# One pool of matrix buffers through four graph layers, with the next layer's masks requested at the last head

## The chip, the cores and the metric

The kernel runs on one core of a Trainium2 chip. The metric is the device time of one execution in microseconds (us). Timed runs before the change took 3488.3, 3495.0 and 3485.93 us; their median is 3488.3 us. One execution was also recorded with the hardware profiler. It took 3488.49 us, and its span from the first to the last instruction is 3486.7 us.

The engines are called as in the profile: PE multiplies matrices and transposes, DVE, ACT and POOL work on tensors elementwise, and SP only issues DMA transfers. Each of them carries out its own list of instructions in order; an instruction that waits for a semaphore holds back what is behind it in that list.

## The reference, cut to what matters

There are N = 3327 nodes with D = 512 features and a dense adjacency matrix. Four layers follow each other, each one with a normalisation and a ReLU ahead of it and a residual behind it:

```python
# layers 0, 1, 2: graph attention with 8, 4 and 8 heads
h = maximum(layernorm(x), 0)
Wh = h @ W                                        # per head
e = leaky_relu(s1[i] + s2[j], 0.2)                # s1 = Wh . a1, s2 = Wh . a2
e = where(adj[i, j] > 0, e, -9e15)                # layer 1: adj + identity, -inf
x = x + elu(softmax(e, axis=j) @ Wh)
# layer 3: mean over the neighbours
h = maximum(layernorm(x), 0)
agg = mask @ h / maximum(deg, 1)
x = x + relu(concat(h @ W_self + b_self, agg @ W_nb + b_nb) @ W_comb + b_comb)
```

## The kernel before, in words

**Attention without exponentials of a matrix.** A leaky ReLU has two slopes, so exp(e) of an edge is one of two products, each of a factor of the row i and a factor of the column j. Which one holds depends on the sign of s1[i] + s2[j]. So a head needs, for each block of 128 source nodes by 128 target nodes, two matrices of zeros and twos in fp8: the edges of one sign and those of the other. Those of one sign come from a compare of the score row with a value per partition (line 683 on ACT, for some blocks line 680 on DVE), combined bit by bit with the adjacency mask (line 687, `and`, on DVE). Those of the other sign are the mask without the first (line 689, `xor`). PE multiplies both with the rows of Wh, which are scaled with the factors of the column and split into three bf16 pieces (lines 794 and 797). In layer 1 (4 heads) one matrix serves after the other in the same buffer (line 822 flips it in place); some groups there are cast to fp32r (line 652: three groups at a time on ACT or DVE, tiles `ts` and `tv`) and multiplied at line 787, the others at line 790.

**Loops.** The 26 tiles of 128 nodes are taken in chunks of 4 target tiles (seven chunks, the last with 2). Within a chunk the loop runs over heads, within a head over five groups of source tiles (6, 6, 6, 4 and 4). For each chunk, head and group there is one pair of matrix buffers, called `tht` and `gt`. In layers 0 and 2 there are seven of each, 3072 bytes per partition; layer 1 has ten `tht`, used for both signs. At the end of a head DVE sums the pieces out of PSUM (lines 812 and 808), and lines 828 to 835 normalise into the tile `A`. After the last head of a chunk, `finish` does the ELU (lines 892, 893 on ACT, 894 on DVE), adds the residual on POOL (895) and stores the rows (896).

**The next layer's projection** is interleaved with the attention as hooks. A node tile goes through stages: normalise (lines 347, 351 on DVE, 352 to 354 on POOL, ReLU at line 359 on ACT), transpose on PE (line 138) with a copy out of PSUM on ACT (line 142), multiply with the weights (line 415; 490 for the last layer), exponentials (446, 449) and scaling (454), splitting into pieces (386, 390, 397, 399; in layer 1 also 470 and 473), and a store of the pieces by SP (line 551). Scores of a whole chunk are transposed and sent at lines 519 and 521. The last chunk's two tiles have no other chunk to hide behind: their stages stand at the joint between two layers. At the joints of layers 0 to 1 and 1 to 2 the kernel also multiplies two weight matrices for the last layer (class `Fusion`): POOL loads a block (line 183) into one of two `xt` buffers, PE transposes (138) and multiplies it (190), ACT copies the result back into that buffer (191), and POOL stores it to `X` (192). Line 204 multiplies the biases.

**Masks and scores.** SP loads the adjacency masks of a chunk (line 273), five tiles out of a pool of six buffers; it loads the score row of a head, broadcast over the partitions (line 695, two buffers), and the pieces of the next head (lines 733 and 739). Within a layer the next chunk's masks are requested one head ahead. The first masks of layers 1 and 2 and of the last stage are requested when that layer begins (lines 703 and 1028). The next layer's first score row is requested at the last head already (line 723).

**The last stage** (lines 1041 to 1057) multiplies the mask, cast to fp32r into one of six `mf` buffers (line 1044 on ACT, 1042 on DVE), with the projected rows `y2_0` to `y2_4`, each in two parts (line 1047), and adds the other terms. The `y2` tiles are loaded by POOL (line 868); `y2_0` has a pool of its own and is requested before layer 2 ends.

**What sets the order.** The kernel's program is written as if for one sequence; a scheduler of the tile framework then arranges the instructions of each engine, from its own estimate of when they can run, and puts in the semaphore waits that data and reused buffers need. `after(inst, name)` (line 145) adds an order without a wait. Tiles live in pools. The attention pools of the layers are opened one after the other at the same addresses, so the first tiles of a layer can wait for whichever tile of the former layer lay there. A scheduler's order for the changed kernel can therefore differ from the former one also far from the lines that were edited.

Of the kernel before, what the change touches and what calls it, by code (L numbers as in the profile page):

```python
# [25 lines left out]
F32 = mybir.dt.float32  # L26
# [11 lines left out]
P = 128  # L38
# [14 lines left out]
def tile_gnn(ctx: ExitStack, tc: tile.TileContext, x, adj, W0, a01, W1, al, ar, W2, a2,  # L53
# [209 lines left out]
    def mask_view(c, g):  # L263
        nt, nj = chunks[c][1], JG[g][1]
        m = mk.tile([P, PER * JM * P], FP8, name="m")
        return m[:, :nt * nj * P].rearrange("p (k j i) -> p k j i", k=nt, j=nj)

    def mask_tiles(c, self_loops=False):
        t0, nt = chunks[c]
        tiles, loops = [], []  # L270
        for g, (j0, nj) in enumerate(JG):
            v = mask_view(c, g)
            nc.sync.dma_start(v, maskd[c][g])
# [250 lines left out]
    def node_stages(L, t, get_x, pool, first=False):  # L524
# [24 lines left out]
        def send():  # L549
            for to, pt in L.to_store:  # L550
                nc.sync.dma_start(to, pt)
            L.to_store = []
            send_s1(L, t, pool, first)
# [138 lines left out]
    def score_rows(l, t0, nt, h):  # L692
# [3 lines left out]
        return v  # L696

    def attention(L, hooks, open_next, close):

        l = L.l  # L700
        H, DA, AO, HW = dims(l)
        DK = DA - 1
        masks = mask_tiles(0, l == 1) if l else masks0
        for c, (t0, nt) in enumerate(chunks):
# [3 lines left out]
            for h in range(H):  # L708
# [37 lines left out]
                for g in range(len(JG)):  # L746
                    if g in early:
                        pv, gv = early.pop(g)
                    else:

                        pt = mp.tile([P, PER * JM * P], FP8, name="tht", bufs=10 if l == 1 else 7)
                        gt = pt if l == 1 else mp.tile([P, PER * JM * P], FP8, name="gt", bufs=7)
                        pv, gv, words, steps = matrices(L, nt, h, g, s1v, masks[g], pt, gt)
                        for step in steps:
                            step()
                        if l == 1:
                            flip.append(words)
                    th[0].append(pv)
                    th[1].append(gv)
                R = mp.tile([P, PER, 2, DA], F32, name="R", bufs=1)  # L760
                deg = l == 0 and h == 0
# [162 lines left out]
    with tc.tile_pool(name="first", bufs=1) as fp:  # L924
# [47 lines left out]
        while hooks.small:  # L972
            hooks.small.pop(0)()
    A, R = [("A", D, F32, n) for n in A_BUFS], ("R", PER * 2 * 129, F32, 1)
    ab, gt, tht = ("ab", JM * 400, BF16, 7), ("gt", PER * JM * P, FP8, 7), ("tht", PER * JM * P, FP8, 7)
    tags = [[A[0], ("R", PER * 2 * 65, F32, 1), tht, ("tr", JM * P, BF16, 5), ("abx", 4 * 400, BF16, 4), gt],
            [A[1], ("ab", JM * 258, F32R, 7), R, ("ts", 2 * JM * P, F32R, 3), ("tv", 2 * 4 * P, F32R, 2), tht[:3] + (10,)],
            [A[2], ab, ("R", PER * 2 * 65, F32, 1), tht, gt]]
    hooks.masks = in_steps([mask_steps(ip, t, g) for t, g in order[20:]])
# [31 lines left out]
    with tc.tile_pool(name="agg", bufs=1, reuse_waits="tile") as op:  # L1011


        y2n = [(f"y2_{g}", nj * 2 * D, F32R, 1) for g, (_, nj) in enumerate(JG)]
        lay_out(op, ("y1", D, F32, 3), ("xo", D, F32, 3), ("o", D, F32, 3), y2n[4], ("gap", 40 * 1024, FP8, 1),
                y2n[3], ("mf", JM * P, F32R, 6), y2n[1], y2n[2])
        rows = {}
# [493 lines left out]
```

## Time and profile before

| What | us or share |
|---|---|
| median of the timed runs | 3488.3 |
| profiled execution, its own time | 3488.49 |
| span of the profiled execution | 3486.7 |
| mean granted clock of PE | 0.994 |
| busy: DVE | 2635.9 (76%) |
| busy: POOL | 625.9 (18%) |
| L683 on ACT, 2448 compares of form `gt` | 1448.3, 677 ns each |
| L687 / L689 on DVE, 557 of each | 448.0 / 446.9, 805 / 803 ns each |
| L1047 on PE, 1352 | 309.6 busy |

PE's matmuls are pipelined, so the duration of one (248 ns for line 794) is longer than the time from one start to the next; on the timeline line 794 and line 797 start every 84 ns, line 790 every 164 ns, line 1047 every 227 ns. An idle time in brackets on a timeline line is the time in which the engine did nothing before that line, with the instruction that ended it behind the arrow. "xN" says how often the instruction was repeated in the line. The granted clock is the share of full speed that the throttle allowed to PE.

Layer 0 runs until about 1180 us, layer 1 until about 2025 us, layer 2 until about 3142 us, and the last stage to the end.

### The profile page before, as it was taken

Reading aid. Unit: us, or ns where it says so; the run is one execution under the profiler, and the core shown is the slowest. Engines: PE = TensorE matmul, PEld = TensorE weight load, DVE = VectorE, ACT = ScalarE, POOL = GpSimd, SP = SyncE. Lnnn points to the kernel's source line nnn. Section 1 sums busy time; section 2 is a strip of 40 time slices with the busy share of each in tenths; the row PEclk is TensorE's granted clock in tenths of the full one; section 3 lists DMA queues with packets and bytes.
Section 4 is the critical chain, followed back from the end, with each engine's and each line's share of the span. In section 5 each row is a group of like instructions: output and inputs, shape, how many; then the busy total and the mean of one; then the engine's idle time right before and its main releaser. Section 6 shows DMA issues by size and latency. Waiting matters only on the chain. (4 is left out here: it accounts for less than half of the span.)

```text
span 3486.7 us, 77621 instructions
## 1 busy us (share of the span) xinstructions
PE 3419.4 (98%) x30751; PEld 3095.4 (89%) x30751; DVE 2635.9 (76%) x5227; ACT 2501.2 (72%) x4113; POOL 625.9 (18%) x858
## 2 busy tenths in 40 slices
PE   8899999999999999999999999999999999999999
PEld 6799999999999788888888879989898989886887
DVE  7888888888878799889988867867676768672221
ACT  6777888878878888988888767766676767572111
POOL 7601222112111202223223320000000001020000
PEclk9999999999999999999999999999999999999999
DMA  8799999999857887877777876655555555586331
GB/s 230 234 287 263 249 257 256 262 266 262 251 178 271 271 285 262 294 266 270 276 273 267 334 261 200 197 179 172 191 171 180 186 176 186 164 296 261 103 107 57
DMA packets 398117, 797.70 MB, mean 229 GB/s; under 512 B 112969, under 2 KB 221844, under 8 KB 397104
## 3 DMA queue, kind: packets, MB, share of 16 engines
q1 hardware_dynamic: 363890, 723.14, 65.3%
q0 software_dynamic: 28128, 62.42, 7.5%
q10 hardware_dynamic: 5726, 7.08, 0.6%
q8 instruction: 245, 4.01, 0.5%
q14 instruction: 128, 1.05, 0.1%
HBM read 663.59 MB, written 129.64 MB: 228 GB/s over the span
## 5 line engine op out<-in xcount | busy, mean ns | idle before, releaser
L683 ACT ACTIVATE gt<-s1b,ks 128x512 fp8e4<-128x512 f32 (+1 forms) x2448 | 1448.3, 677 | 376.0 <-PE acc L797 260.6
L794 PE MATMUL acc<-ab,tht 128*128 128x195 bf16 (+1 forms) x9112 | 1550.6, 248 | 5.9 <-DVE tht L687 4.6
L797 PE MATMUL acc<-ab,gt 128*128 128x195 bf16 (+1 forms) x9112 | 1549.8, 248 | 2.5 <-DVE gt L689 2.3
L797 PEld LDWEIGHTS <-gt 128*128 128x128 fp8e4 x10744 | 1052.0, 98 | 26.4 <-issue 18.2
L794 PEld LDWEIGHTS <-tht 128*128 128x128 fp8e4 x10744 | 1051.9, 98 | 23.0 <-DVE tht L687 9.1
L687 DVE TENSOR_TENSOR tht<-gt,m 128x768 uint32<-128x768 uint32 (+3 forms) x557 | 448.0, 805 | 103.0 <-ACT gt L683 99.4
L689 DVE TENSOR_TENSOR gt<-tht,m 128x768 uint32<-128x768 uint32 (+3 forms) x557 | 446.9, 803 | 9.4
L652 ACT CAST ts<-tht 128x1536 fp32r<-128x1536 fp8e4 x208 | 302.2, 1472 | 100.3 <-PE acc L787 93.8
L680 DVE TENSOR_SCALAR gt<-s1b,ns 128x512 fp8e4<-128x512 f32 (+1 forms) x446 | 223.8, 505 | 161.1 <-PE acc L797 160.3
L787 PE MATMUL acc<-ab,ts 128*128 128x258 f32 x2496 | 332.8, 289 | 1.6 <-DMA ab<-ab 1.5
L787 PEld LDWEIGHTS acc<-ab,ts 128*128 128x128 f32 x2496 | 312.0, 189 | 9.7 <-ACT e L893 1.9
L895 POOL TENSOR_TENSOR xt<-xt,e 128x512 f32<-128x512 f32 x72 | 120.7, 1676 | 1066.2 <-DVE e L894 1005.8
L683 ACT ACTIVATE tht<-s1b,ks 128x512 fp8e4<-128x512 f32 (+1 forms) x504 | 309.1, 681 | 0.7
L1047 PE MATMUL acc<-y,mf 128*128 128x512 f32 x1352 | 309.6, 391 | 0.0
L1047 PEld LDWEIGHTS acc<-y,mf 128*128 128x128 f32 x1352 | 253.6, 188 | 55.8 <-issue 0.5
L794 PE MATMUL acc<-abx,tht 128*128 128x195 bf16 (+1 forms) x1632 | 284.6, 248 | 3.4 <-DVE tht L687 3.3
L797 PE MATMUL acc<-abx,gt 128*128 128x195 bf16 (+1 forms) x1632 | 284.4, 248 | 3.2 <-DVE gt L689 1.6
L812 DVE TENSOR_REDUCE R<-acc 128x130 f32<-128x390 f32 x416 | 214.3, 554 | 89.8 <-PE acc L797 86.8
L1044 ACT CAST mf<-m 128x768 fp32r<-128x768 fp8e4 (+1 forms) x78 | 59.1, 762 | 243.2 <-PE acc L1047 231.4
L790 PE MATMUL acc<-ab,tht 128*128 128x387 bf16 x1248 | 223.8, 327 | 6.4 <-DMA ab<-ab 4.2
L787 PE MATMUL acc<-ab,tv 128*128 128x258 f32 x1664 | 218.2, 283 | 0.0
L787 PEld LDWEIGHTS acc<-ab,tv 128*128 128x128 f32 x1664 | 207.2, 189 | 0.6 <-DVE tv L652 0.2
(163 smaller groups left out, 3706.9 us busy)
## 6 DMA issues: line engine op xcount, KB each, us to landing
ab<-ab SPq DMA_DIRECT2D x333, 600.0 KB, 5.8
ab<-ab SPq DMA_DIRECT2D x112, 774.0 KB, 6.7
ab<-ab SPq DMA_DIRECT2D x112, 516.0 KB, 5.4
ab<-ab SPq DMA_DIRECT2D x112, 400.0 KB, 3.8
abx<-ab SPq DMA_DIRECT2D x110, 400.0 KB, 6.5
ab<-ab SPq DMA_DIRECT2D x56, 582.0 KB, 6.2
s1b<-s SPq DMA_DIRECT2D x120, 256.0 KB, 5.5
m<-mask SPq DMA_DIRECT2D x69, 384.0 KB, 4.0
```

The costliest lines, as they stand in the source:

```text
L652: (nc.scalar.copy if KIND[g] == "s" else nc.vector.tensor_copy)(t[:, :k1 - k0, :nj], th[a][g][:, k0:k1])
L680: nc.vector.tensor_scalar(gv[:, :, jj, :], s1v, L.ns2[:, j, h:h + 1], 2.0, op0=ALU.is_gt, op1=ALU.mult, saturate=False)
L683: nc.scalar.activation(gv[:, :, jj, :], s1v, AF.Relu, bias=L.ks2[:, j, h:h + 1], scale=BIG, saturate=False)
L687: nc.vector.tensor_tensor(pu, gu, mu, ALU.bitwise_and)
L689: nc.vector.tensor_tensor(gu, pu, mu, ALU.bitwise_xor)
L787: mm = nc.tensor.matmul(acc[k][:, :2 * DA], thr[g][:, k - ks[0], jj, :], ab[a][g][:, jj, :], start=(j == 0), stop=(j == NT - 1), skip_grou ...
L790: mm = nc.tensor.matmul(acc[k][:, :3 * DA], th[a][g][:, k, jj, :], ab[a][g][:, jj, :3 * DA], start=(j == 0), stop=(j == NT - 1), skip_grou ...
L794: nc.tensor.matmul(acc[k][:, :3 * DA + o], th[0][g][:, k, jj, :], ab[0][g][:, jj, :3 * DA + o], start=(j == 0), stop=False, skip_group_che ...
L797: mm = nc.tensor.matmul(acc[k][:, AO:AO + 3 * DA + o], th[1][g][:, k, jj, :], ab[0][g][:, jj, AO:AO + 3 * DA + o], start=False, stop=(j == ...
L812: nc.vector.tensor_reduce(R[:, k], v.rearrange("p a (s d) -> p a d s", s=3), AX.X, ALU.add)
L895: nc.gpsimd.tensor_add(xt, xt, e)
L1047: nc.tensor.matmul(acc[k], mf[:, jj, :], y2[g][:, jj, s, :], start=(j0 + jj == 0 and s == 0), stop=(j0 + jj == NT - 1 and s == 1))
```

## The change

All layers and the last stage take their matrices from one pool, `mats`, of ten buffers `th` of 3072 bytes per partition; it lies on the other side of the memory and is never closed until the end. In layers 0 and 2 the pairs count in a cycle of seven: five pairs take two `th` buffers each, and two pairs take one of two double buffers `tx` in the layer's own pool. Layer 1 uses the ten `th` only, and the last stage uses them as `mf`. The other tiles of the layers' pools and of the last stage's are laid out at other addresses. The masks of the next layer are requested at the last head of the last chunk, right after its matrices, in layers 0 and 1. The last stores of the next layer's pieces (line 551) are put behind the last of these mask requests in order.

```diff
+            lds.append(nc.sync.dma_start(v, maskd[c][g]).ins.name)
...
-                nc.sync.dma_start(to, pt)
+                st = nc.sync.dma_start(to, pt)
+                if "masks" in early:
+                    after(st, lds[-1])
...
+    pairs = [0, 0, 0]
...
-        masks = mask_tiles(0, l == 1) if l else masks0
+        masks = early.pop("masks") if l else masks0
...
-                        pt = mp.tile([P, PER * JM * P], FP8, name="tht", bufs=10 if l == 1 else 7)
-                        gt = pt if l == 1 else mp.tile([P, PER * JM * P], FP8, name="gt", bufs=7)
+                        s = PER * JM * P
+                        if l == 1:
+                            pt = gt = thp.tile([P, s], FP8, name="th", bufs=10)
+                        elif (pairs[l] + (4 if l == 0 else 0)) % 7 < 5:
+                            pt, gt = [thp.tile([P, s], FP8, name="th", bufs=10) for _ in range(2)]
+                        else:
+                            both = mp.tile([P, 2 * s], FP8, name="tx", bufs=2)
+                            pt, gt = both[:, :s], both[:, s:]
+                        pairs[l] += 1
...
+                if last and h == H - 1 and l < 2:
+                    early["masks"] = mask_tiles(0, l == 0)
...
-    tags = [[A[0], ("R", PER * 2 * 65, F32, 1), tht, ("tr", JM * P, BF16, 5), ("abx", 4 * 400, BF16, 4), gt],
-            [A[1], ("ab", JM * 258, F32R, 7), R, ("ts", 2 * JM * P, F32R, 3), ("tv", 2 * 4 * P, F32R, 2), tht[:3] + (10,)],
-            [A[2], ab, ("R", PER * 2 * 65, F32, 1), tht, gt]]
+    thp = main.enter_context(tc.tile_pool(name="mats", bufs=1, side="right", reuse_waits="tile"))
+    lay_out(thp, ("th", PER * JM * P, FP8, 10))
+    A, R, R1 = [("A", D, F32, n) for n in A_BUFS], ("R", PER * 2 * 65, F32, 1), ("R", PER * 2 * 129, F32, 1)
+    tx = ("tx", 2 * PER * JM * P, FP8, 2)
+    tags = [[A[0], R, ("tr", JM * P, BF16, 5), ("abx", 4 * 400, BF16, 4), tx],
+            [A[1], ("ab", JM * 258, F32R, 7), R1, ("ts", 2 * JM * P, F32R, 3), ("tv", 2 * 4 * P, F32R, 2)],
+            [("ab", JM * 400, BF16, 7), R, tx, ("gap", 800, FP8, 1), A[2]]]
...
-        lay_out(op, ("y1", D, F32, 3), ("xo", D, F32, 3), ("o", D, F32, 3), y2n[4], ("gap", 40 * 1024, FP8, 1),
-                y2n[3], ("mf", JM * P, F32R, 6), y2n[1], y2n[2])
+        lay_out(op, ("y1", D, F32, 3), ("xo", D, F32, 3), ("o", D, F32, 3), y2n[4], ("gap", 31136, FP8, 1),
+                y2n[1], y2n[2], y2n[3])
...
-                        mf = op.tile([P, JM, P], F32R, name="mf", bufs=6)
+                        mf = thp.tile([P, PER * JM * P], FP8, name="th", bufs=10).bitcast(F32R)
+                        mf = mf.rearrange("p (j i) -> p j i", j=JM)
```

Line numbers in the text are those of the kernel before.

More of the change, by code (lines that the diff above doesn't have):

```diff
@@ L266, in mask_view @@
         return m[:, :nt * nj * P].rearrange("p (k j i) -> p k j i", k=nt, j=nj)
+    lds = []
     def mask_tiles(c, self_loops=False):
@@ L272, in mask_tiles @@
             v = mask_view(c, g)
-            nc.sync.dma_start(v, maskd[c][g])
+            lds.append(nc.sync.dma_start(v, maskd[c][g]).ins.name)
             if self_loops:
@@ L973, in tile_gnn @@
             hooks.small.pop(0)()
-    A, R = [("A", D, F32, n) for n in A_BUFS], ("R", PER * 2 * 129, F32, 1)
-    ab, gt, tht = ("ab", JM * 400, BF16, 7), ("gt", PER * JM * P, FP8, 7), ("tht", PER * JM * P, FP8, 7)
-    tags = [[A[0], ("R", PER * 2 * 65, F32, 1), tht, ("tr", JM * P, BF16, 5), ("abx", 4 * 400, BF16, 4), gt],
-            [A[1], ("ab", JM * 258, F32R, 7), R, ("ts", 2 * JM * P, F32R, 3), ("tv", 2 * 4 * P, F32R, 2), tht[:3] + (10,)],
-            [A[2], ab, ("R", PER * 2 * 65, F32, 1), tht, gt]]
+    thp = main.enter_context(tc.tile_pool(name="mats", bufs=1, side="right", reuse_waits="tile"))
[5 more added lines that the diff above has]
+            [("ab", JM * 400, BF16, 7), R, tx, ("gap", 800, FP8, 1), A[2]]]
     hooks.masks = in_steps([mask_steps(ip, t, g) for t, g in order[20:]])
```

## The prediction

> **What bounds the kernel now.** I read the page first, then busy time by windows of 50 us, then PE's list of waits, then the timelines of PE, ACT and POOL at the three joints between layers. The page says that PE sets the time:
>
> ```profile
> PE 3419.4 (98%) x30751; PEld 3095.4 (89%) x30751; DVE 2635.9 (76%) x5227; ACT 2501.2 (72%) x4113; POOL 625.9 (18%) x858
> ...
> PE 41%; ACT 0%; DVE 0%; POOL 0%; issue 0%; POOLq 0%
> ```
>
> Of a span of 3486.7 us PE is busy 3419.4 (the first figure), so about 67 us is all that better order can win, and the chain of waits (last line) holds next to nothing but PE. The windows tell where the 67 us lie. Columns: stretch and length, then busy us of PE, PEld, DVE, ACT, POOL, then granted clock, DMA share, GB/s.
>
> ```profile
> 1150.00:1200.00 50.00, 46.96 (x380) 38.87 (x378) 31.46 (x82) 34.30 (x78) 9.74 (x16) 1.00 0.85 284
> 2000.00:2050.00 50.00, 42.93 (x234) 32.20 (x233) 29.61 (x58) 24.78 (x42) 17.25 (x27) 0.97 0.87 318
> 2100.00:2150.00 50.00, 50.00 (x597) 50.00 (x595) 39.25 (x77) 36.40 (x60) 0.00 (x0) 1.00 0.65 207
> 3150.00:3200.00 50.00, 48.71 (x175) 33.30 (x176) 8.53 (x19) 9.35 (x14) 4.24 (x9) 0.93 0.81 311
> ```
>
> The third is a middle of a layer: PE never idle. So are nearly all windows. PE idles 3.0 us at the joint of layers 0 and 1, 5.2 + 7.1 at that of 1 and 2, 2.1 + 1.3 at the last stage; also 25.3 between 50 and 350 us (start of layer 0) and about 8 after its last matmul. The clock column adds a second loss: 0.97 over 50 us is 1.5 us, 0.93 is 3.5 us. What ended PE's idle time:
>
> ```profile
> PE tp L138 <- ACT h L359: 12.1, 5, 8.9
> PE acc L794 <- DVE tht L687: 7.9, 4, 3.4
> PE acc L790 <- DMA ab<-ab: 4.2, 2, 2.6
> PE acc L790 <- DVE tht L687: 2.1, 1, 2.1
> ```
>
> The columns are total us, times, longest. Waits for `tht L687` are those for the first matrices of a layer, which the change can bring forward: one of 2.1 (layer 1) and the longest, 3.4 (layer 2).
>
> **Middle of the layers: 0.** Every engine issues as many instructions after as before, of the same shapes. Five of seven pairs in the shared pool and two in `tx` make the same seven pairs in flight as seven `tht` and seven `gt` did; layer 1 has ten as before. One semaphore more on each of the 557 pairs (row L687 x557), at the 17 ns of the shortest such row (POOL's semaphore instructions at L192), would be 9.5 us of a queue; it is hidden because ACT is ahead: before L683 it idles 376.0 us, 260.6 of them until PE gives a buffer back. Bounds 0 to +9.5; I take 0, by the PE rows without idle time.
>
> **Joint 0 to 1: +1.6.** Today ACT stands idle while layer 1's compares could run:
>
> ```profile
> 1166.08 2.89 ACT L683 ACTIVATE gt<-s1b,ks 128x256 fp8e4<-128x256 f32 x7
> 1179.02 1.07 ACT L142 COPY hT<-tp 128x512 f32<-128x512 f32 x2 [4.90 <-PE tp L138]
> 1192.86 3.77 ACT L683 ACTIVATE tht<-s1b,ks 128x512 fp8e4<-128x512 f32 x6
> ```
>
> The first is the last of layer 0, the third the first of layer 1: it waited behind relu and copies in ACT's order. In the order of the changed kernel 18 of these compares (3.77/6 = 0.63 us each, 11.3 us) stand between the first and the second line. From 1168.97, with two L470 (1.2), L521 (0.3) and some waiting of the L470s (1.3 today), ACT reaches L142 at about 1182. PE needs that copy for the Fusion's L190, which today starts at 1179.66 after 0.24 idle. So the 2.12 us stall at L790 goes, and one of about 2.5 us comes at L190. What is late next: DVE puts layer 1's L687 and L680 between the final L812 and L835, so A is ready about 3.6 us later; PE's transpose of h comes 2.5 later itself and today has 1.7 to spare, so that is nearly hidden. Three L652 casts (1.472 us each, page) then stand ahead of the second L142, and PE's last L415 waits about 1.5, less the ten more L790 (164 ns apart) that it can do first. Sum: -2.1 + 2.5 + 1.2 = +1.6; bounds -2 (L142 in time) to +5 (waits of 3.1 and 1.5 whole, and one drop of the clock at 2.5, the middle of the two losses above).
>
> **Joint 1 to 2: +1.3.** Masks of groups 1 to 4 are asked for on SP at about 2016.7, 5.5 us earlier, ahead of two L551 stores, which go 3.5 us later (the four requests) at no cost, since the load of their group waits for a later L551 at 2051.95 in any case. So L683, L680 and L687 run earlier. The 3.37 us stall goes. But POOL's order changes as well. Today:
>
> ```profile
> 2031.70 0.57 POOL L192 DMA_DIRECT2D X<-xt  x1
> 2034.34 0.26 POOL L354 TENSOR_SCALAR mv<-mv 128x1 f32<-128x1 f32 x1
> 2038.54 0.56 POOL L183 DMA_DIRECT2D xt<-in_L_gnn_W_nb_dram  x1 [1.77 <-PE tp L138]
> 2040.70 0.26 POOL L354 TENSOR_SCALAR mv<-mv 128x1 f32<-128x1 f32 x1
> ```
>
> L183 reloads the buffer that L192 stores, so it waits until that store has landed; POOL is in order, so L352 to L354 of the next tile wait behind it. Now only the second tile does. In the changed order the L183 stands before the first tile's L352 to L354, and a second one before the second's. Landing of L192:
>
> ```profile
> DMA to landing us min/median/max: 2.5/4.5/7.2
> ```
>
> With the median of 4.5, L183 goes at 2036.5, L354 ends near 2039 (about 1.6 from L352 to L354, an L192 of 0.6 between) and h near 2039.8, where PE today starts L138 at 2037.01 without waiting: a new idle of some 2.5 us. From there: L138 0.6, copy 0.7, L415 3.83, so the second L138 is done at 2045.2. Its h is ready at 2044.3 (the second L183 waits for a store of 2037.1 that lands at 2041.6). On ACT four L683, L446, L449 and one more L683 stand between that h and L142 (5 x 0.63 + 0.2 = 3.4), so the copy ends at 2048.2 and PE's second L415 starts there; today it starts at 2046.94. That is +1.3, with the 3.37 us stall gone and its time spent elsewhere. L808 to L835 end 1.8 us later too, behind L687 and L689 (0.95 each), which the wait for X covers. Bounds by the same chain: landings of 2.5 bring L415 to 2044, -3; two landings of 6.3, the store's own today, +5; a clock drop more costs 1.5 to 3.5 above that.
>
> **Joint 2 to 3: -1.3.** ACT idles 12.47 us before L892 at 3143.41. The last stage's casts (L1044 six times, L1042 four times) fit there, since `mf` now comes from a pool that is free as layer 2 ends. Ten L1047 (0.227 us apart, 2.27 us) come between the transposes, where PE idles 2.09 + 0.68 + 0.62 = 3.4. They need y2_0, whose load at L868 was issued at 3138.93 and landed at 3150.1, so the first three wait as long as h does today, and hold up L138 by 0.7. Bounds: +3 (y2_0 later beside three mask loads that are now earlier) to -5 (idle 3.4 and some of the clock's 3.5 gone).
>
> **Start of layer 0 and the rest: 0.** One L689 comes before the last L812, which takes a 1.5 us stall and lengthens a 0.8 one; the third row of scores is issued about 6 us later, behind W loads, and ACT has up to seven pairs in hand (1.4 heads of 17.5 us) to hide it. Without that cover it costs up to 5; bounds -3 to +5. The stalls on `ab` (4.2, 1.5) and the 8 us at the end stay, as SP's order there stays.
>
> Sum: 0 + 1.6 + 1.3 - 1.3 + 0 = +1.6. The profiled execution took 3488.49 us (the span and 1.8 around it), 0.2 above the median of 3488.3. Forecast 3488.5 + 1.6 = **3490.1**.
>
> **The clock.** The rows: 0.97 and 0.93 in windows with idles of 1.9 to 3.4 us, 1.00 in the one with 2.12. The Trainium skill, "TensorE: Matmul & The Clock Gate", Part 1, says the rate halves after idle gaps over about 3.4 us. By it only the 3.37 us stall would be at risk, and taking it away would bring an estimated 1.7 us besides (half of 3.4), so 3488.4. The window with 0.93 holds no idle longer than 2.09 us, so the rows speak against that threshold; I count a stall of 2 us or more, old or new, as one that may drop the clock, expect as many drops after as before, and keep 3490.1.
>
> **Rivals.** *All as wished*: stalls 2.12 + 3.37 + 2.09 + 0.68 + 0.62 = 8.9 go, nothing new comes, and the clock keeps 1.5 + 3.5: -13.9, so 3474.6. For it: ACT has the idle time. Against it: the new places of L683 and L183 in queues that are in order. *Queues cost more* (slower): the same work ahead of what PE waits for, at L142 on ACT and L183 on POOL, at the upper bounds +5 and +5 + 3.5, with the last stage at 0: +13.5, so 3502.0. It decides from where X's stores take over 6 us to land and both new idles drop the clock; below that the loss stays under 10 us. *It does nothing*: each earlier matrix meets a wait of the same end (h, y2_0, X): 3488.5.
>
> **Chances.** Forecast 0.46 (3484 to 3497), nothing 0.12, all as wished 0.19, queues 0.23. A run of this kernel tells no change from about 0.3%, 10.5 us. So faster 0.19, same 0.58, slower 0.23. The range takes in most of both rivals: 3475 to 3503.
>
> **What would show it.** At 0 to 1, the 2.12 at L790 gone and an idle PE before L190: right; L190 at 1179.7 and no stall after: my joint was too dear. At 1 to 2, L138 waiting for h with L183 ahead of L352 on POOL; if L183 doesn't wait there, the gain is real. At 2 to 3, L1047 between the transposes, ended by y2_0's DMA. Any idle PE in a middle window would refute the zero there and make the forecast wrong by up to 9.5.

## The result: 0.66% slower, 10 us beyond the range

| | before | after |
|---|---|---|
| median of six timed runs each, us | 3489.91 | 3513.01 |
| lowest to highest, us | 3485.93 to 3495.0 | 3508.88 to 3515.22 |
| after / before, 95% interval | | 1.0066 [1.0056, 1.0077] |
| profiled execution / its span, us | 3488.49 / 3486.7 | 3510.98 / 3509.2 |
| PE idle (span less busy), us | 67.3 | 77.9 |

In the kernel after, lines move down: the compare L683 is L687, L680 is L684, `and` L687 is L691, `xor` L689 is L693, L794/L797 are L809/L812, L790 is L805, L617 is L621, L828 is L843, L352 to L354 are L354 to L356, L359 is L361, L415 is L417, L490 is L492, L1047 is L1065, L868 is L883. The experiments' kernels are off by a few lines more. The page of the kernel after, its busy engines, the shares of its chain of waits, and the group of the last stage's matmuls:

```profile
PE 3431.3 (98%) x30751; PEld 3099.2 (88%) x30751; DVE 2629.8 (75%) x5227; ACT 2502.3 (71%) x4113; POOL 639.3 (18%) x858
...
PE 40%; DVE 0%; POOL 0%; ACT 0%; issue 0%; POOLq 0%
...
L1065 PE MATMUL acc<-y,th 128*128 128x512 f32 x1352 | 315.5, 395 | 3.4 <-DVE mv L353 3.4
```

PE still sets the time, with the same 30751 matmuls. It is busy 11.9 us longer for them, and 5.9 of those are in the last group, which was 309.6 before: the same 1352 matmuls take longer, which is no waiting at all. What ended PE's idle time (total, times, longest):

```profile
PE acc L809 <- DVE th L691: 10.5, 3, 7.3
...
PE mm L417 <- ACT hT L142: 4.3, 4, 2.8
PE mm L190 <- ACT hT L142: 3.9, 2, 3.6
...
PE acc L805 <- DMA ab<-ab: 2.4, 2, 2.0
```

The waits for layer 2's and layer 1's first matrices (3.4 and 2.1) are gone as wished. New are one of 7.3 for a matrix, and waits for the copy L142. The windows of the kernel after (columns as in the prediction):

```profile
150.00:200.00 50.00, 41.43 (x444) 39.60 (x444) 34.10 (x75) 37.84 (x66) 10.32 (x16) 0.90 0.87 268
1150.00:1200.00 50.00, 46.36 (x410) 40.29 (x408) 38.94 (x99) 44.79 (x102) 7.93 (x13) 0.93 0.82 273
2050.00:2100.00 50.00, 43.05 (x328) 35.21 (x329) 27.05 (x61) 30.09 (x55) 10.44 (x17) 0.93 0.59 203
2100.00:2150.00 50.00, 50.00 (x597) 50.00 (x595) 38.64 (x74) 35.54 (x58) 0.00 (x0) 1.00 0.60 199
3150.00:3200.00 50.00, 46.62 (x222) 30.92 (x220) 15.36 (x39) 10.77 (x16) 8.12 (x14) 0.97 0.88 335
3300.00:3350.00 50.00, 50.00 (x217) 40.43 (x216) 9.82 (x17) 9.16 (x12) 0.00 (x0) 1.00 0.32 101
```

And two of the kernel before:

```profile
150.00:200.00 50.00, 46.11 (x512) 43.95 (x511) 42.32 (x91) 45.14 (x80) 11.39 (x16) 1.00 0.94 284
3300.00:3350.00 50.00, 50.00 (x220) 41.02 (x219) 11.16 (x18) 9.97 (x13) 0.00 (x0) 1.00 0.34 106
```

From 150 to 200 us PE does 444 matmuls instead of 512, at a clock of 0.90 instead of 1.00. The middle of layer 2 is full. At 3300 PE is busy throughout in both kernels and yet does 217 instead of 220.

To place the loss, I took the start of the same matmul in both traces at several points; the difference grows as follows.

| stretch | us | forecast |
|---|---|---|
| start of layer 0, to 660 us | +9.6 | 0 |
| joint 0 to 1 | +2.0 | +1.6 |
| joint 1 to 2 | +5.8 | +1.3 |
| joint 2 to 3 | -1.8 | -1.3 |
| last stage, pace of L1065 | +4.8 | none |
| landing of the last store | +2.1 | none |
| span | +22.5 | +1.6 |

The same 22.5 by kind: PE idles 10.6 us more and is busy 11.9 longer. Of the 11.9, about 4.8 are pace, and the other 7 the clock, which was at half rate for 54.6 us instead of 34.2 (the clock's records without the end; half of the 20.4 more is 10.2, some of it while PE idled). The landing of the last store is scatter: it landed 8.2 us after its issue, 6.1 before, and 6.2 in an experiment with the same end.

How far two traces of one order can differ is seen from an experiment below (`b_align`), in which the kernel before has only its last stage's addresses moved. Up to there nothing is edited, and yet its trace stands at +2.0 by 660 us, +5.3 by 1317 and +5.8 in layer 2. So the +2.0 of joint 0 to 1 and the -1.8 of joint 2 to 3 can't be told from scatter by one trace. The start of layer 0 can: the kernel after and the six experiments that edit nothing there stand at +9.2 to +14.6 by 660. So can joint 1 to 2: five kernels with the order of the kernel after lose 5.8 to 7.9 there, `b_align` 0.5.

**Start of layer 0.** Timeline of ACT in the kernel after:

```profile
166.96 3.77 ACT L687 ACTIVATE th<-s1b,ks 128x512 fp8e4<-128x512 f32 x6
178.64 0.72 ACT L687 ACTIVATE tx<-s1b,ks 128x512 fp8e4<-128x512 f32 x1 [7.91 <-DMA s1b<-s]
179.27 0.53 ACT L621 ACTIVATE cpm<-cpm 128x416 f32<-128x416 f32 x1
```

DVE and PE behind it:

```profile
179.83 0.70 DVE L843 TENSOR_TENSOR R<-R,cpm 128x520 f32<-128x520 f32 x1 [7.34 <-ACT cpm L621]
180.52 0.95 DVE L691 TENSOR_TENSOR th<-th,m 128x768 uint32<-128x768 uint32 x1
...
181.53 0.51 PE L809 MATMUL acc<-ab,th 128*128 128x195 bf16 x2 [7.27 <-DVE th L691]
```

Before, ACT had this order:

```profile
165.51 6.22 ACT L683 ACTIVATE gt<-s1b,ks 128x512 fp8e4<-128x512 f32 x10
172.23 0.55 ACT L617 ACTIVATE cpm<-cpm 128x416 f32<-128x416 f32 x1 [0.50 <-DVE cpm L616]
172.69 6.83 ACT L683 ACTIVATE gt<-s1b,ks 128x512 fp8e4<-128x512 f32 x11
180.62 1.95 ACT L683 ACTIVATE gt<-s1b,ks 128x512 fp8e4<-128x512 f32 x3 [1.10 <-DMA s1b<-s]
```

The score row of head 2 is no later than before: SP asks for it at 172.66 (174.75 before), and the compare that waits for it starts at 178.64 (180.62 before). Before, ACT had the exponential L617 and eleven more compares ahead of the first that needs this row. After, the scheduler has put the first compare that needs it (into `tx`) ahead of the exponential and of compares of head 1. ACT waits 7.91 for a transfer, DVE 7.34 for the exponential, and PE 7.27 for a matrix that could have been made in time.

**Joint 0 to 1**, ACT and then PE:

```profile
1181.10 4.39 ACT L687 ACTIVATE th<-s1b,ks 128x512 fp8e4<-128x512 f32 x7
...
1185.54 5.62 ACT L687 ACTIVATE th<-s1b,ks 128x512 fp8e4<-128x512 f32 x9
1191.06 1.03 ACT L142 COPY hT<-tp 128x512 f32<-128x512 f32 x2
```

```profile
1191.67 6.01 PE L190 MATMUL mm<-w,hT 128*128 128x512 f32 x7 [3.64 <-ACT hT L142]
```

**Joint 1 to 2**, POOL and then PE:

```profile
2048.29 0.54 POOL L183 DMA_DIRECT2D xt<-in_L_gnn_W_nb_dram  x1 [0.40 <-issue]
2048.82 0.54 POOL L192 DMA_DIRECT2D X<-xt  x1
...
2057.03 0.56 POOL L183 DMA_DIRECT2D xt<-in_L_gnn_W_nb_dram  x1 [4.07 <-DMA X<-xt]
...
2058.65 0.26 POOL L356 TENSOR_SCALAR mv<-mv 128x1 f32<-128x1 f32 x1
```

```profile
2051.69 0.65 PE L138 MATMUL tp<-ident,h 128*128 128x128 f32 x4 [1.87 <-ACT h L361]
...
2059.81 0.66 PE L138 MATMUL tp<-ident,h 128*128 128x128 f32 x4 [1.27 <-ACT h L361]
...
2063.53 5.51 PE L417 MATMUL mm<-w,hT 128*128 128x264 f32 x16 [2.81 <-ACT hT L142]
```

**Joint 2 to 3**, PE:

```profile
3168.64 0.94 PE L1065 MATMUL acc<-y,th 128*128 128x512 f32 x3 [3.38 <-DVE mv L353]
3169.42 0.60 PE L138 MATMUL tp<-ident,h 128*128 128x128 f32 x4
3169.77 1.76 PE L1065 MATMUL acc<-y,th 128*128 128x512 f32 x4
```

Here the named releaser, DVE, had long been done: the load of `y2_0`, asked for at 3156.3, landed at 3168.5. The idle is as long as the three of the kernel before together (3.38 for 2.09 + 0.68 + 0.62); what is shorter is the stretch at half rate behind it, 3.4 us for 6.8, and half of that difference is 1.7 us.

### The profile page after: what moved, and what is told of

Its sections match the earlier page's. It is cut to its first block, busy times and chain, and to the rows that moved or that the text cites. A ratio compares the mean times of both kernels' runs of the same rounds, so it can differ in the third digit from the quotient of the medians.

```text
span 3509.2 us, 77653 instructions
## 1 busy us (share of the span) xinstructions
PE 3431.3 (98%) x30751; PEld 3099.2 (88%) x30751; DVE 2629.8 (75%) x5227; ACT 2502.3 (71%) x4113; POOL 639.3 (18%) x858
## 5 line engine op out<-in xcount | busy, mean ns | idle before, releaser
L687 ACT ACTIVATE th<-s1b,ks 128x512 fp8e4<-128x512 f32 (+1 forms) x2248 | 1346.2, 678 | 270.5 <-PE acc L809 268.0
L809 PE MATMUL acc<-ab,th 128*128 128x195 bf16 (+1 forms) x6484 | 1112.3, 248 | 7.3 <-DVE th L691 7.3
L812 PE MATMUL acc<-ab,th 128*128 128x195 bf16 (+1 forms) x6484 | 1111.4, 248 | 0.7 <-DVE th L693 0.6
L809 PEld LDWEIGHTS <-th 128*128 128x128 fp8e4 x7660 | 750.4, 98 | 20.1 <-DVE th L691 11.2
L812 PEld LDWEIGHTS <-th 128*128 128x128 fp8e4 x7660 | 750.4, 98 | 19.5 <-issue 12.3
L691 DVE TENSOR_TENSOR th<-th,m 128x768 uint32<-128x768 uint32 (+3 forms) x537 | 433.4, 809 | 162.2 <-ACT th L687 156.6
L687 ACT ACTIVATE tx<-s1b,ks 128x512 fp8e4<-128x512 f32 (+1 forms) x704 | 423.9, 677 | 123.5 <-PE acc L812 83.5
L809 PE MATMUL acc<-ab,tx 128*128 128x195 bf16 (+1 forms) x2628 | 454.8, 248 | 1.3 <-DVE deg L830 0.9
L812 PE MATMUL acc<-ab,tx 128*128 128x195 bf16 (+1 forms) x2628 | 454.7, 248 | 0.4 <-DVE tx L693 0.4
L656 ACT CAST ts<-th 128x1536 fp32r<-128x1536 fp8e4 x208 | 302.1, 1472 | 100.3 <-PE acc L802 94.3
L693 DVE TENSOR_TENSOR th<-th,m 128x768 uint32<-128x768 uint32 (+3 forms) x397 | 316.1, 796 | 8.6 <-DMA tr<-at 4.1
L1065 PE MATMUL acc<-y,th 128*128 128x512 f32 x1352 | 315.5, 395 | 3.4 <-DVE mv L353 3.4
L812 PEld LDWEIGHTS <-tx 128*128 128x128 fp8e4 x3084 | 301.9, 98 | 10.2 <-issue 8.5
L1065 PEld LDWEIGHTS acc<-y,th 128*128 128x128 f32 x1352 | 253.9, 188 | 64.1 <-issue 4.7
L684 DVE TENSOR_SCALAR th<-s1b,ns 128x512 fp8e4<-128x512 f32 (+1 forms) x542 | 268.4, 513 | 55.9 <-PE acc L809 53.7
L809 PEld LDWEIGHTS <-tx 128*128 128x128 fp8e4 x3084 | 302.0, 98 | 5.2 <-issue 3.1
L805 PE MATMUL acc<-ab,th 128*128 128x387 bf16 x1248 | 226.5, 331 | 2.4 <-DMA ab<-ab 2.4
```

The source lines that it names most:

```text
L656: (nc.scalar.copy if KIND[g] == "s" else nc.vector.tensor_copy)(t[:, :k1 - k0, :nj], th[a][g][:, k0:k1])
L684: nc.vector.tensor_scalar(gv[:, :, jj, :], s1v, L.ns2[:, j, h:h + 1], 2.0, op0=ALU.is_gt, op1=ALU.mult, saturate=False)
L687: nc.scalar.activation(gv[:, :, jj, :], s1v, AF.Relu, bias=L.ks2[:, j, h:h + 1], scale=BIG, saturate=False)
L691: nc.vector.tensor_tensor(pu, gu, mu, ALU.bitwise_and)
L693: nc.vector.tensor_tensor(gu, pu, mu, ALU.bitwise_xor)
L805: mm = nc.tensor.matmul(acc[k][:, :3 * DA], th[a][g][:, k, jj, :], ab[a][g][:, jj, :3 * DA], start=(j == 0), stop=(j == NT - 1), skip_grou ...
```

## The experiments

The theory after the result: the loss is *order and layout*, no lack of buffers. New pools gave the scheduler other orders in in-order queues (start of layer 0, joints 0 to 1 and 1 to 2), each new stall of 2 us or more may drop the clock, and `y2` and the last stage's matrices lie at addresses that slow L1065. Rivals: the early mask requests cost it; buffers really come free later; `mf` must be in its own pool. Each experiment changes the kernel after, unless it says otherwise; of each edit only the lines that matter are shown. Positions in time ("by 1317") give how much later than before the same matmul starts; the kernel after has +9.6 by 660, +11.6 by 1317, +17.4 in layer 2, +20.4 at the last matmul.

**The exponential first, in layer 0.**

```diff
+                if l == 0 and h == 2 and hold:      # first chunk
+                    after(cp, L.cx)                 # L.cx: the exponential, L621
```

> The changed kernel with one order added and nothing else: in layer 0's first chunk the compares of head 2 come behind the exponential of the row factors (line 617 of before) on ACT. Theory 'order in the queues': the 7.3 us stall of PE near 181 us is that exponential, held on ACT behind a compare that waits for head 2's score row; it shrinks to about 1 us and the clock drops of the start get fewer, so by 430 us the kernel is about 7 to 9 us earlier than the changed one: about 3504. Rival 'buffers': the matrices wait for buffers of the shared pool that really are free late; the stall stays within 1 us and the time at 3513. Rival 'masks': the early request costs the time; nothing moves here.

Measured: 3511.26, ratio 1.0060 [1.0043, 1.0077]; +8.9 at the start of layer 0. ACT, then PE:

```profile
173.09 0.55 ACT L621 ACTIVATE cpm<-cpm 128x416 f32<-128x416 f32 x1 [0.19 <-DVE cpm L620]
180.73 2.56 ACT L687 ACTIVATE tx<-s1b,ks 128x512 fp8e4<-128x512 f32 x4 [7.09 <-DMA s1b<-s]
183.20 1.32 ACT L687 ACTIVATE th<-s1b,ks 128x512 fp8e4<-128x512 f32 x2
```

```profile
187.40 0.67 PE L811 MATMUL acc<-ab,th 128*128 128x195 bf16 x3 [7.29 <-DVE th L693]
```

A miss. The exponential is early again, and the stall is as long: the compares of head 1 into `th` (third ACT line) still stand behind the one that waits. Not the exponential is what matters, but the first instruction that waits for the row.

**All compares of head 2 behind head 1's**, on ACT and DVE.

```diff
+                if l == 0 and hold and h == 2:
+                    after(cp, L.cp[1])              # and the same for DVE's compares
```

> The changed kernel with one order added in layer 0's first chunk: head 2's compares, on ACT and DVE, come behind the last compare of head 1 (and so the exponential of the row factors comes ahead of them too). Theory 'order in the queues': what held PE 7.3 us near 181 us, with the exponential moved as well, is a compare of head 2 that waits for its score row ahead of head 1's matrices on ACT. Now PE's stall at that place is under 1.6 us, as in the kernel before, and by 230 us PE is 1 to 3 us behind the kernel before instead of 5.8; by 430 us 2 to 4 instead of 8.7: about 3506. Rival 'buffers': head 1's matrices wait for buffers of the shared pool that are really freed late; a stall of 5 us or more stays, about 3511.

Measured: 3511.79, 1.0056 [1.0041, 1.0072]. The stall at 181 is gone, but one of 7.34 has come at 221. SP, DVE, PE:

```profile
200.62 6.70 SPq L331 DMA_DIRECT2D w<-in_L_gnn_W_dram  x5
...
212.20 1.19 SPq L238 DMA_TRANSPOSE tr<-at  x1
```

```profile
219.28 0.43 DVE L244 TENSOR_SCALAR st<-tr 128x512 fp8e4<-128x512 bf16 x1 [7.48 <-DMA tr<-at]
...
220.24 0.95 DVE L697 TENSOR_TENSOR th<-th,m 128x768 uint32<-128x768 uint32 x1
```

```profile
221.25 0.35 PE L815 MATMUL acc<-ab,th 128*128 128x195 bf16 x1 [7.34 <-DVE th L697]
```

The same mechanism in another queue: a mask transpose asked for late, behind loads of W on SP, is waited for by a DVE instruction with `and` behind it. With one order mended, the scheduler has made another.

**Another start of layer 0's cycle of seven**, with both joints mended and addresses aligned (below) in both kernels. Five pairs in `th` come first, instead of the two in `tx` after one pair:

```diff
-    (pairs[l] + (4 if l == 0 else 0)) % 7 < 5
+    (pairs[l] + (0 if l == 0 else 0)) % 7 < 5
```

> The kernel with both orders at the joints and the aligned last stage, and one number changed: layer 0's cycle of seven pairs starts at 0 instead of 4, so other pairs take tx; pool, buffers and addresses are the same. In the order the scheduler then writes, all compares of head 1 stand ahead of head 2's on ACT, and the exponential ahead of most. Theory 'order in the queues': PE's loss at the start of layer 0, 8 us by 228 us and 13 by 467 us in the kernel with the other start, falls to under 3 us: median 3489 to 3493, against 3499.5. Rival 'buffers': the shared pool lies where the first projections' rows, pieces and scores lay, its first buffers are free late whatever the order; the loss stays above 7 us: 3497 to 3501.

Measured: 3492.22, 0.9997 [0.9988, 1.0006], against 3499.47, 1.0022 [1.0011, 1.0033], for the same kernel with the old start: 7.3 us. Its profiled execution (3498.56) was its slowest; it has lost 0.7 us by 228, where the other start had lost 8.4. The longest wait for a matrix on PE there, 3.2 for 7.3:

```profile
174.42 0.75 PE L812 MATMUL acc<-ab,th 128*128 128x195 bf16 x4 [3.21 <-DVE th L694]
```

The number and size of buffers, and the pairs in flight, are the same. The edit also moves the first use of `tx` from the second pair to the sixth; but in the kernel after ACT's wait ahead of `tx` was ended by the row's transfer (7.91 <-DMA s1b<-s), not by a buffer. So the stall of 7.3 us is one of order, and "buffers come free later" falls as its cause. What follows it isn't explained by this: the same trace has lost 8.6 us by 660, where the other start had lost 14.2.

**No early request of masks.**

```diff
-                if last and h == H - 1 and l < 2:
-                    early["masks"] = mask_tiles(0, l == 0)
-        masks = early.pop("masks") if l else masks0
+        masks = mask_tiles(0, l == 1) if l else masks0
```

> The changed kernel without the early request: the masks of the next layer are asked for at its beginning, as before; pool and layouts stay. Theory 'order in the queues': the early start of the next layer's compares comes from the free buffers of the shared pool, which the scheduler sees, so the stalls at L190 between layers 0 and 1 and around L138 between 1 and 2 stay, and so does the start of layer 0 (where no request differs): 3508 to 3515. Rival 'masks': the request moves SP's and DVE's work ahead and makes the loss at the joints; without it 5 to 8 us come back, 3505 to 3508, and the loss at the start of layer 0 and in the last stage stays.

Measured: 3508.54, 1.0051 [1.0034, 1.0068]. By 1317 +14.8, in layer 2 +19.1, at the last matmul +19.8. By the medians 4.5 of the 23 us could be the request's, but the two intervals overlap, and the two joints are hardly better without it: +3.0 and +4.3, for +2.0 and +5.8 with it. So the rival "masks" falls as the main cause of the loss; the last version below keeps the request and is faster than the kernel before.

**The joints.** Three kernels. The first orders ACT: a layer's first compares behind the Fusion's second copy L142.

```diff
+            stored["fused"] = copied[-1]            # after the two fusion.block calls
+                if l and h == 0 and hold:
+                    after(cp, stored["fused"])
```

> The changed kernel with one order added: the first compares of layers 1 and 2 on ACT come behind the copy (line 142) of the Fusion's second block. Theory 'order in the queues', ACT's part: at the joint of layers 0 and 1 PE's 3.6 us stall before L190 shrinks under 0.5 us and the half clock after it goes; the loss there, 3.0 us in the changed kernel's trace, becomes 0 or a gain of up to 3; at the joint of 1 and 2, where POOL's loads stay in place, 3 to 5 us of loss stay. About 3506 to 3510. Rival 'buffers': next layer's first matrices are then late for their own first matmuls and the 2 to 3 us come back as stalls on L687: 3512.

The second orders POOL: the loads L183 of blocks 3 and 4 behind the last tile's L354 to L356.

```diff
-                fusion.load(k, gone[-1])
+                fusion.load(k, mvs[-1])             # mvs: the names of L356
```

> The changed kernel with another order added: the loads of the Fusion's third and fourth block on POOL (line 183) come behind the last tile's normalisation (lines 352 to 354). Theory 'order in the queues', POOL's part: at the joint of layers 1 and 2 PE no longer waits 1.9 and 1.3 us for h at L138, the loss there falls from 5.7 to 1 to 3 us; the stall at L190 between layers 0 and 1 stays: 3508 to 3511. Rival: the matmuls of the third and fourth block now wait for their later loads instead, and nothing is gained: 3513.

The third has both, and the last stage's rows aligned (below).

> Both orders at the joints, and the last stage with all masks and y2 rows at 224 modulo 256 bytes (a pad of 192 ahead of y2_4, the gap 160 smaller). Theory 'order and alignment': all five groups of the last stage run at 226.7 ns (-7.2 us against the changed kernel), the joints give 4 to 9 us back, the start of layer 0 keeps its loss of about 9: 3497 to 3502. If the median of the kernel with all orders, 3496.6, came from head 2's order, this one is 5 us or more above it; if that order brought nothing, as its own run says (3511.8), this one is at 3496 or below.

Measured: 3509.06, 1.0056 [1.0038, 1.0073]; 3507.83, 1.0045 [1.0030, 1.0060]; 3499.47, 1.0022 [1.0011, 1.0033]. PE in the first, at both joints:

```profile
1201.91 6.84 PE L417 MATMUL mm<-w,hT 128*128 128x260 f32 x16 [2.98 <-ACT hT L142]
...
2055.68 1.11 PE L138 MATMUL tp<-ident,h 128*128 128x128 f32 x4 [3.90 <-ACT h L361]
```

In the second:

```profile
1195.49 4.97 PE L191 MATMUL mm<-w,hT 128*128 128x512 f32 x7 [4.09 <-ACT hT L142]
...
2054.30 0.66 PE L138 MATMUL tp<-ident,h 128*128 128x128 f32 x4 [1.88 <-ACT h L362]
```

The first takes the wait at L190 away and gets 2.98 at the second tile's copy instead, so that joint 0 to 1 gains nothing (+4.8 from the start of layer 0 to 1317); POOL's wait at joint 1 to 2 stays. The second leaves L190's wait (now 4.09) and loses nothing from 1317 to layer 2 (+15.4 at both); its first wait for h is as long as in the kernel after (1.88 for 1.87), and what is gone are the 1.27 and the 2.81 behind it. With both, the joints cost nothing that one trace can tell: +14.2 after the start of layer 0, +13.6 by 1317, +13.2 in layer 2. Whether head 2's order brings something in the kernel with all edits, which the third expectation asks, stays open: 3499.47 lies between its two values. What is left there is the start of layer 0. The queues that the prediction named, ACT at the first joint and POOL at the second, are the right ones; each needs its own order.

**`mf` in the last stage's own pool again.**

```diff
-                        mf = thp.tile([P, PER * JM * P], FP8, name="th", bufs=10).bitcast(F32R)
+                        mf = op.tile([P, JM, P], F32R, name="mf", bufs=6)
```

> The changed kernel, but the last stage's fp32r masks come from six buffers of the stage's own pool again, at addresses below y2_1 as in the kernel before; the gap is smaller by what they take, so y2_0 stays where the changed kernel has it and y2_3 lies lower. Theory 'addresses': the start-to-start time of the last stage's matmuls (227 to 233 ns in the kernel before, by group; 228 to 233 in the changed one) goes with where masks and y2 lie, so the mean falls from 232 to near 228.5 and the stage gets 4 to 6 us shorter, with 1 to 3 us lost at the joint of layers 2 and 3, where the masks can't be cast early: about 3510. Rival 'other traffic': the pace comes from what ACT, DVE and the DMAs do beside PE, which is the same; the mean stays at 232 ns and the time at 3513 to 3516.

Measured: 3513.48, 1.0070 [1.0053, 1.0087]. L1065's mean pace, start to start within a group and from the second chunk on, by source group 0 to 4: 233.3, 230.2, 226.7, 226.7, 235.1 ns. Before it was 233.3, 228.5, 226.7, 226.7, 226.7 (mean 228.7), after 231.2, 233.4, 233.2, 233.1, 228.3 (mean 232.0); 3.3 ns x 1352 is 4.5 us. Two groups are fast again and two still slow, so that the shared pool as such isn't the cause: the pace goes by group, and so by the address of `y2_g`. The time is in the rival's range, the pace isn't; the start of layer 0, where nothing was edited, is +14.6 in this execution.

**Addresses alone.** Two kernels of 2704 and 3072 such matmuls with nothing beside them; neither computes a part of the reference. The first puts weights and rows in every pair of 13 stretches of 16 KB.

> No part of the model is computed (the output is zeros): 13 by 13 blocks of 16 fp32r matmuls (128 by 128 weights, 128 by 512 moving), the weights in one 16 KB stretch of each partition and the moving rows in another, with no other engine at work. Theory 'addresses': some pairs of stretches run at 226 to 227 ns from start to start and others at 232 to 234, and the pairs of the two kernels (weights at 134 to 153 thousand with rows at 153 to 202 thousand: fast; with rows at 205 to 229 thousand: slow; weights at 199 to 229 thousand with rows at 108 to 174 thousand: slow) come out as in the traces. Rival 'other traffic': all 169 pairs agree within 1 ns.

All pairs took 226.6 to 226.7 ns: the stretch has no effect. All of these addresses agree modulo 256. The second varies both in steps of 32 bytes within 256.

> No part of the model is computed (the output is zeros): 8 by 8 blocks of 48 fp32r matmuls of the last stage's shape, with no other engine at work; the weights start at 0, 32, ... 224 bytes past a multiple of 128 and the moving rows likewise. Theory 'alignment': blocks with equal residues modulo 128 run at 226.7 ns, others at 228 to 235. Rival 'other traffic': all 64 blocks agree within 1 ns.

Mean ns from start to start, over the second half of each block; a row is the start of the weights, a column that of the moving rows, in bytes past two addresses that are equal modulo 256:

```
        0     32     64     96    128    160    192    224
  0  226.7  233.3  228.8  233.3  233.3  234.2  233.3  233.3
 64  233.3  233.3  226.7  233.3  228.8  233.3  233.3  234.2
224  233.4  228.7  233.3  233.3  234.3  233.3  233.3  226.7
```

The other five rows are the same, shifted, within 0.6 ns. Equal starts modulo 256 give 226.7, moving rows 64 bytes further 228.8, all else 232.7 to 234.5. The expectation had 128 for the period; starts 128 apart take 233.3, so it is 256. This explains the groups: before, `mf` lay at 32, `y2_0` at 224 (233.3), the others at 32; after, `th` lies at 224, three of the `y2` at 192 (233), the last at 32, which is 64 further (228.3); with `mf` back in its pool, `mf` and `y2_1` to `y2_3` lie at 192, `y2_0` at 224 and `y2_4` at 32. A group has 8 or 12 matmuls there, and a slow group's pace goes on for up to ten in the next; that makes the mixed means (`y2_0` after: 231.2 at equal starts, behind `y2_4`; and 228.0 below).

**Aligning in the kernels.** First a pad of 64 bytes ahead of `y2_4`:

```diff
+        lay_out(op, ..., ("pad", 64, FP8, 1), y2n[4], ("gap", 31104, FP8, 1), y2n[1], y2n[2], y2n[3])
```

> The changed kernel with a pad of 64 bytes ahead of y2_4 and a gap 32 bytes smaller in the last stage's pool, nothing else: now y2_0 to y2_4 and the masks in th all start at 96 modulo 128 bytes. Theory 'alignment': a matmul's pace falls from 233 to 227 ns where weights and moving rows start at another residue modulo 128; all five groups run at 226.7 ns, the mean falls from 232.0 to 226.7, and the last stage is 1352 x 5.3 ns = 7 us shorter than in the changed kernel: about 3505. Rival 'place' (which stretch of the partition they lie in, beside other traffic): moving them by 32 and 64 bytes changes nothing, 232.0 ns, 3512.

Measured: 3508.73, 1.0051 [1.0035, 1.0066]; pace 228.0, 226.7, 226.7, 226.7, 232.7. Groups 1 to 3 as expected; `y2_4` came to lie at 96 and slowed. In the kernel before, with 192 bytes, all are equal:

```diff
-        ("o", D, F32, 3), y2n[4], ...
+        ("o", D, F32, 3), ("pad", 192, FP8, 1), y2n[4], ...
```

> The kernel before with a pad of 192 bytes ahead of y2_4 and nothing else, so that masks and all y2 rows start at 224 modulo 256 bytes. Theory 'alignment': group 0 falls from 233.3 to 226.7 ns and group 1 from 228.5 to 226.7, so the last stage is 312 x 8.4 ns = 2.6 us shorter, the rest is the same: 0.9992 of the kernel before. Rival 'place': the pace of group 0 stays at 233.3 and the time is equal.

Measured: 226.7 in all groups, the last stage 2.3 us shorter in the trace; the whole time, 3490.6 against 3492.3, is 0.9993 [0.9984, 1.0002], not to be told from no change. One window of it, to compare with the two at 3300 above:

```profile
3300.00:3350.00 50.00, 50.00 (x222) 41.42 (x221) 10.14 (x17) 9.15 (x12) 0.00 (x0) 1.00 0.35 108
```

222 matmuls where the kernel before had 220 and the one after 217, all at the clock of 1.00 and with PE busy.

**All edits together**, head 2 and the joints ordered and the pad of 64:

> The changed kernel with all orders at once and the aligned last stage: head 2's compares behind head 1's; at the joints the next layer's first compares behind the Fusion's second copy on ACT, and the loads of its last two blocks behind the last tile's normalisation on POOL. Theory 'order and alignment': against the changed kernel -5 at the start of layer 0, -2 to -5 at the joint of layers 0 and 1 (no 3.6 us stall at L190 and no clock drop there), -3 to -6 at that of 1 and 2, -7 in the last stage: 3490 to 3495, 0 to 5 us above the kernel before. Rival 'buffers and traffic': only the ends of the queues move, the waits come back elsewhere: 3505 or more.

Measured: 3496.56, 1.0011 [1.0002, 1.0020]. About 16 of the 23 us are back by the medians, 19 by the ratios. Its profiled execution was its slowest (3506.32) and has a stall of 7.86 at 223, so the start of layer 0 is still the place.

**A version from these findings**: both joints ordered, all rows aligned, and layer 0 with its own seven `tht` and `gt`, the shared pool opened from layer 1 on.

```diff
+            if l == 0:
+                pt = mp.tile([P, s], FP8, name="tht", bufs=7)
+                gt = mp.tile([P, s], FP8, name="gt", bufs=7)
```

> Both orders at the joints, the aligned last stage, and layer 0 with seven tht and seven gt in its own pool as in the kernel before; the shared pool is opened at layer 1. Both theories expect no loss at the start of layer 0 (within 1.5 us of the kernel before until 1100 us), where the order of ACT, DVE and SP is that of the kernel before. At the joint of layers 0 and 1 the first matrices lie on layer 0's last ones, so 0 to +2 there; -0.4 at 1 and 2, -2 to -3 at 2 and 3, -2.7 in the last stage: 3485 to 3489, 3 to 6 us under the kernel before. If the loss at the start came from anything that the early masks or the joints' orders do, it is still there: 3497 or more.

Measured: 3485.54, 0.9984 [0.9975, 0.9993] against 3492.0 of the same hours: faster than both kernels, if only by 0.16%. PE:

```profile
305.35 0.26 PE L815 MATMUL acc<-ab,tht 128*128 128x196 bf16 x1 [1.83 <-DVE tht L694]
...
1194.91 0.83 PE L811 MATMUL acc<-ab,th 128*128 128x387 bf16 x4 [1.17 <-DVE th L694]
...
2049.22 5.51 PE L418 MATMUL mm<-w,hT 128*128 128x264 f32 x16 [1.95 <-DVE AB L457]
...
3151.47 0.94 PE L1074 MATMUL acc<-y,th 128*128 128x512 f32 x3 [2.32 <-DMA y<-y]
```

From 140 us to the end of layer 0 no stall is over 1.83 us here (2.23 before). At joint 0 to 1 the 2.12 of the kernel before is 1.17; at joint 1 to 2 the 3.37 is gone, and the longest new wait is one of 1.95 at 2049. Against the kernel before the trace stands at -1.8 by 660, +0.1 by 1317, +1.3 in layer 2 and -3.8 at the last matmul. At the last stage the load of `y2_0` still ends a wait.

## Why the prediction was wrong

- **Start of layer 0: 0, bounds -3 to +5. This step failed**: +9.6. I looked at the `xor` L689 and at the row of scores on SP, and took "up to seven pairs in hand" as cover. I did not look at where ACT's order had put the first compare that needs that row. The pairs in hand were never made, because their compares stood behind it; and the exponential, for which DVE waits, stood there too. The row that stood later "behind W loads" was another one: asked for at 209.28 after and at 197.61 before, while head 2's was asked for at 172.66 and 174.75. The prediction's own list had a hint: it called the waits for `tht L687` those for the first matrices of a layer, but three of the four at L794, 4.5 of their 7.9 us, stood at 238, 307 and 317, at the start of layer 0. That order is the cause of the 7.3 us stall is shown (its wait ends with the row; another start of the cycle takes 7.3 us off the median, and pools of layer 0's own lose nothing there); why the scheduler chose this order is not. Of the +9.6, 5.8 are there by 228 us; the rest comes with single stalls up to 660, whose cause stays open.
- **Joint 0 to 1: +1.6, measured +2.0.** The 2.12 at L790 went, the idle came at L190 (3.64 for 2.5), after 16 of the 18 compares counted, and one stretch of 6.8 us at half rate followed; a stall on `ab` that had been 2.64 became 0.39, so the sum fits by luck, and +2.0 is within the scatter of one trace.
- **Joint 1 to 2: +1.3, measured +5.8**, inside its bound of 5 + 3.5. The chain was right, its sizes weren't. The store of X ahead of the first L183 landed within some 4 us, so the first tile lost 1.87, not 2.5; but the store issued at 2048.82 took 7.6 us to land, where the sum had the median of 4.5. So the second L183 stood 4.07 and held the second tile as well (1.27, then 2.81 at L417), and the clock fell twice.
- **Joint 2 to 3: -1.3, measured -1.8**, with L1065 between the transposes and `y2_0`'s load as the end of the wait, as written. But no idle was won: the three became one of 3.38. The gain is that of the clock (1.7 us), which the sum had not counted, so it fits by luck: the kernel with `mf` back in its own pool has three idles of 2.10 + 0.68 + 0.62 there, and without a stretch at half rate it gains 2.9.
- **Middle of the layers: 0**, right; the window of 2100 to 2150 is full in both kernels, and the difference stays at +9.6 from 660 to 1100, near +11.7 from 1317 to 1900 and at +17.4 from 2110 to 3140.
- **Last stage: not a term.** "Of the same shapes" was taken to mean of the same duration: +4.8. The row of L1047 alone could not have told; its two paces by group could, had I looked at one start after another.
- **The clock: "as many drops after as before" failed.** The 20.4 us more of half rate make 7 to 10 of the 22.5, spread over the rows above. The reading that a stall of 2 us may drop the clock held. Whether one does is not set by its length: the stalls of 2.12 and 2.64 us that left the clock alone in the kernel before, at 1198 and 1267, are 2.14 and 2.40 in `b_align` and dropped it both times.
- The rival *queues cost more* has the right mechanism and sign at the joints; it lacked layer 0's start and the pace, and so stopped at +13.5.

Left open: why the scheduler orders so; the single stalls between 350 and 900 us, which differ between kernels that are not edited there (+9.2 to +14.6 at the end of layer 0); and when exactly a stall drops the clock.

## What to carry to other kernels

When pools or buffer names change, compare the new order on every in-order queue from the first instruction on, and look above all for one that waits for a transfer and has moved ahead of work that is ready. A stall costs its length, and the lower clock behind it can cost nearly as much again (3.64 us at L190, then 6.8 us at half rate, which is 3.4). Where TensorE is the bound, equal shapes don't mean equal time: look at the pace from start to start, by operand.

## What was new about the hardware

- **Start addresses modulo 256 set the pace of these fp32r matmuls**: 226.7 ns when weights and moving rows agree, up to 234.5 when not, 3.4%, at full granted clock. The reason isn't known. The Trainium skill, "TensorE: Matmul & The Clock Gate", section Back-to-back issue gap, gives N/2.4 + 2.5 for an isolated matmul, an estimate of 216 ns at N = 512; no run here of this type was below 226.6, and the formula has no term for addresses.
- **The clock fell after stalls of 1.87 and 2.81 us**: in the kernel after at 2054.0, behind the one of 1.87 that ended at 2051.69 and one of 0.68 at 2053.02, and at 2064.2, behind the one of 2.81. Not each stall of 2.1 to 2.6 us did so. A stretch at half rate lasted 3.4, 6.8 or 10.2 us, but for the one at the end of a run.
